# Adding the last sorted tiles of a mixture of experts to their tokens: through DRAM, or by products on chip

## The chip, the cores and the metric

The kernel runs on one core of one Trainium2 chip. The metric is the device time of one execution in microseconds, given as the median of several runs. The engines are PE (TensorE, matrix products), DVE (VectorE), ACT (ScalarE), POOL (GpSimd) and SP (SyncE, which here only issues transfers). Transfers run on the core's 16 DMA engines.

## The reference

The input is 2 sequences of 1024 tokens with 256 features, all in float32. An attention block with 16 heads of 128 (one shared key and value head) is followed by a mixture of experts. Both are modulated by shifts, scales and gates that depend on the sequence. Cut to what matters here:

```python
x = x + ga * attention(layernorm(x) * (1 + ca) + sa)
h = layernorm(x) * (1 + cb) + sb
logits = h @ router_w.T                      # 8 experts
topk_vals, topk_idx = top_k(logits, 2)
topk_w = softmax(topk_vals)
y1 = expert's w1 applied to h                # 2 * 176 columns
y2 = expert's w2 applied to silu(gate) * up  # 256 columns
y = sum over the two experts of topk_w * y2
out = x + gb * y
```

So each of the 2048 tokens has two expert results, which have to be weighted, multiplied by the gate `gb`, brought back to the token's place and added to the token's own row.

## The kernel before, in words

The tokens stand in 16 token tiles of 128 (`NT`), in four blocks of 512 (`NBLK`). `xs[:, t, :]` holds token tile `t` on chip for the whole run. The attention goes block by block, and PE works through 256 steps of a head and a key tile in each. Between these steps hooks, put there by `at(head, step, function)`, hand out the other work. One of them, in block 1, is `clear_sorted`: it fills the DRAM tensor `sorted_x` with zeros through SP's queue and writes into its rows the number of a row that no token owns.

The experts' stage works on sorted rows. Each row of a token (features, its weight in column `WEIGHT`, the row it belongs to in column `TO`) is scattered to `sorted_x`, so that the rows of one expert stand together in tiles of 128. There are `ALL` = 39 such tiles. `SETS` splits the token tiles in two: the first 12, and the last 4, which belong to the last attention block and are known only late. The sorted tiles from `ONES` = 32 on hold rows of the last four token tiles only.

One sorted tile is one object of class `Sorted`. Its stages are `turn` (transpose on PE, copy on ACT), `up` (product with w1, then ACT and DVE), `turn_back` (transpose) and `down` (product with w2). At the end of `down`, DVE evicts the product into `ysb` with weight and gate, and POOL issues an indirect DMA that scatters the 128 rows of `ysb` to the DRAM tensor `results`, two rows for each token. The loop over `m` runs these stages staggered. It takes 2.49 us a tile in the later part, and PE is always busy in it.

When the scatters that a token tile depends on have landed, `fetch` loads its two rows for each token from `results` (256 KB for a token tile). `combine` adds the two rows, adds the token's own row from `xs`, and stores the sum to the output. Scatters write rows of their own, so the class `Scattered` frees them of waits for each other; its `read` makes a load wait for the first `n` scatters. The loads of the first 12 token tiles wait for the first 32 scatters, those of the last 4 for all 39.

The order on each engine is made by a scheduler from the program's order and its own estimates. `tc.issue_after(i)` holds back what stands inside until instruction `i` has been issued on the planner's list. After the loop, five combines of the first set are put beside the last evictions (`BESIDE`). Then POOL, after its last scatter, writes a single column `sent`, and DVE copies it to `seen`. That copy stands ahead of the other seven combines of the first set. The last four loads go out on SP and ACT in turn, and four combines follow them.

Of the kernel before, what the change touches and what calls it, by code (L numbers as in the profile page):

```python
# [43 lines left out]
FP = mybir.dt.float32  # L44
I32 = mybir.dt.int32
AF = mybir.ActivationFunctionType
ALU = mybir.AluOpType
# [3 lines left out]
P = 128  # L51
# [9 lines left out]
def tile_adaln_attention_moe(  # L61
# [15 lines left out]
    nc = tc.nc  # L77
    B, N, D = x.shape
# [6 lines left out]
    QB = 512  # L85
# [9 lines left out]
    TOP = 2  # L95
    SETS = ((0, (NBLK - 1) * QT), ((NBLK - 1) * QT, NT))
# [3 lines left out]
    ONES = TOP * SETS[0][1] + E  # L100
    ALL = (TOP * NT * P + E * (P - 1)) // P
    PARTS = 3

    xt = x.rearrange("b (t p) d -> p (b t) d", p=P)
    ot = out.rearrange("b (t p) d -> p (b t) d", p=P)
# [6 lines left out]
    xs = keep.tile([P, NT, D], FP, name="xs")  # L112


    WEIGHT, TO, BATCH, ROW = D, D + 1, D + 2, D + 4
# [29 lines left out]
    for t in range(QT, TPB):  # L145
# [35 lines left out]
        base=0, channel_multiplier=0,  # L181
# [30 lines left out]
    results = dram.tile([(TOP * NT + ALL) * P, D], FP, name="results")  # L212
# [29 lines left out]
    into_results = Scattered("into_results")  # L242
# [4 lines left out]
    with ExitStack() as attn:  # L247
# [88 lines left out]

        def clear_sorted():

            zero = work.tile([P, ROW], FP, tag="h", name="zero")
            nc.vector.memset(zero, 0.0)  # L340
            by_tile = sorted_x.rearrange("(m p) d -> p m d", p=P)
            nc.sync.dma_start(out=by_tile, in_=zero.unsqueeze(1).to_broadcast([P, ALL, ROW]))
            nobody = work.tile([P, ALL, 1], I32, tag="z", name="nobody")
            nc.gpsimd.iota(nobody, [[P, ALL]], base=TOP * NT * P, channel_multiplier=1)
            with nc.allow_non_contiguous_dma(reason="one number of each row"):
                nc.sync.dma_start(out=by_tile[:, :, TO : TO + 1].bitcast(I32), in_=nobody)
# [175 lines left out]
        TWO = 2  # L522
# [885 lines left out]
        for blk in range(NBLK):  # L1408
# [78 lines left out]
            last = attention(blk, q, steps, besides)  # L1487
# [17 lines left out]
    with ExitStack() as moe:  # L1505
# [42 lines left out]
        class Sorted:  # L1548
# [45 lines left out]
            def down(self):  # L1594
                m = self.m
                at = expert(m) * (2 * D)
                y = ps_y.tile([P, D], FP, tag="y", name=f"sy_{m}")
                for c in range(2):
                    nc.tensor.matmul(  # L1599
                        y,  # L1600
                        self.actT[:, c, :],
                        w2_flat[:, c * D :][:, bass.ds(at, D)],
                        start=(c == 0),
                        stop=(c == 1),
                    )
                ysb = mg.tile([P, D], FP, tag="ysb", name=f"ysb_{m}", bufs=5)
                self.evicted = nc.vector.scalar_tensor_tensor(  # L1607
                    ysb, y, self.x[:, WEIGHT : WEIGHT + 1], self.gate, ALU.mult, ALU.mult
                )
                ins = nc.gpsimd.indirect_dma_start(  # L1610
                    out=results,
                    out_offset=bass.IndirectOffsetOnAxis(
                        ap=self.x[:, TO : TO + 1].bitcast(I32), axis=0
                    ),
                    in_=ysb,
                    in_offset=None,
                )
                self.scattered = ins.ins
                into_results.add(ins)

            def gates(self):

# [9 lines left out]
        def fetch(t, queue=nc.sync):  # L1632

            y = row_buffer(f"y_{t}").rearrange("p (k d) -> p k d", k=TOP)
            load = queue.dma_start(
                out=y,
                in_=results[TOP * t * P : TOP * (t + 1) * P, :].rearrange(
                    "(p k) d -> p k d", k=TOP
                ),
            )  # L1640
            into_results.read(load, ONES if t < SETS[0][1] else ALL)
            return y

        def combine(t, y, queue):

            sum_ = y[:, 0, :]
            nc.vector.tensor_tensor(sum_, sum_, y[:, 1, :], ALU.add)
            nc.vector.tensor_tensor(sum_, sum_, xs[:, t, :], ALU.add)
            queue.dma_start(out=ot[:, t, :], in_=sum_)

        settle.pools(mg, ms, ps_t, "t")
        gb_more = mg.tile([P, D], FP, name="gb_more", bufs=1)
        nc.vector.tensor_tensor(gb_more, gb[:, 1, :], gb[:, 0, :], ALU.subtract)
        tiles = []
        fetched, have = [], 0
        back = done = 0
# [9 lines left out]
            7: [lambda: count(NBLK - 1, mg, ps_t, "t"), lambda: place_second(mg, settle.shares)],  # L1666
        }
        SCATTERS = 8
        LATER = 24
        for m in range(ALL + 3):  # L1670
            there = ALL if m >= SCATTERS + TOP else FULL
            while len(tiles) < min(m + 1 + PRE, there):
                tiles.append(Sorted(len(tiles)))
            for f in late.get(m, ()):
                f()
            if m < ALL:
                tiles[m].turn()
            if 0 <= m - 1 < ALL:
                tiles[m - 1].up()
            sooner = m >= LATER  # L1680
            while back < min(m - 2 + sooner, ALL):
                tiles[back].gates()
                tiles[back].turn_back()
                back += 1
            while done < min(m - 3 + sooner, ALL):
                tiles[done].down()
                done += 1
            if SCATTERS <= m < SCATTERS + TOP:
                k = m - SCATTERS
# [12 lines left out]
        def added(some, behind, queue):  # L1702
            with tc.issue_after(behind):
                for t, y in some:
                    combine(t, y, queue)

        BESIDE = 5
        for i in range(BESIDE):
            m = ALL - 4 + i // 2
            added(  # L1710
                fetched[i : i + 1],
                tiles[m].evicted.ins if i % 2 else tiles[m + 1].active.ins,
                nc.sync,
            )
        sent = mg.tile([P, 1], FP, name="sent", bufs=1)
        with tc.issue_after(tiles[-1].scattered):
            nc.gpsimd.memset(sent, 0.0)
        seen = mg.tile([P, 1], FP, name="seen", bufs=1)
        with tc.issue_after(tiles[-1].evicted.ins):
            look = nc.vector.tensor_copy(seen, sent).ins  # L1720
        lasts = [(t, fetch(t, (nc.sync, nc.scalar)[t % 2])) for t in range(*SETS[1])]
        added(fetched[BESIDE:], look, nc.scalar)
        for t, y in lasts:
            combine(t, y, (nc.sync, nc.scalar)[t % 2])


_OUT = ((2, 1024, 256), "float32")
# [41 lines left out]
```

## Time and profile before

| | us |
|---|---|
| median of 3 runs | 1278.46 (1278.01 to 1279.04) |
| the profiled execution | 1271.44 |
| its span, first to last instruction | 1269.7 |
| PE busy in it | 1244.3 (98%) |
| DVE, ACT, POOL busy | 845.6, 454.2, 188.0 |
| last product of the experts ends | 1254.5 |

The profile is one execution, recorded instruction by instruction. A timeline row gives the start, the duration, the engine with the source line, what was written from what, and in brackets how long the engine had been idle and what ended that. The chain of waits follows the end back from the last instruction to what released each step. A row of a windows table gives the stretch, its length, the busy time of PE, PE's weight loads, DVE, ACT and POOL, then the granted clock of PE, the mean busy share of the DMA engines, and the GB/s that they moved. A transfer has two times: its issue, which is a short instruction of the issuing queue, and its landing.

### The profile page before, as it was taken

The numbers are of one execution on the slowest core, as the hardware profiler recorded it, in microseconds if no ns is written. First come the engines' busy times: TensorE is split into PE (matmuls) and PEld (weight loads), VectorE is DVE, ScalarE is ACT, GpSimd is POOL, SyncE is SP. The second block draws the span as 40 slices with busy tenths as digits, with TensorE's granted clock in tenths as the row PEclk, the third lists the DMA queues.
The fourth block names the chain that finished last, engine by engine and source line by source line (L and its number), as shares of the span: only waits on it lengthen the run. The fifth ranks groups of instructions, "written<-read, shape, count | busy, mean of one in ns | idle before, by whom it ended". The sixth has DMA issues, their size and how long they took to land.

```text
span 1269.7 us, 13438 instructions
## 1 busy us (share of the span) xinstructions
PE 1244.3 (98%) x4116; PEld 681.3 (54%) x4116; DVE 845.6 (67%) x1747; ACT 454.2 (36%) x887; POOL 188.0 (15%) x222
## 2 busy tenths in 40 slices
PE   8999999999999999999999999999999999999995
PEld 4544444457644444448545454448545454467773
DVE  6577789666866766665966666666857775547555
ACT  3533333431233334430333334331433343313431
POOL 3210323110000100000000000000000323203642
PEclk9999999999999999999999999999999999999997
DMA  8011031312011025111011111012011123212426
GB/s 265 0 34 34 9 88 22 91 22 72 7 43 52 30 94 142 34 34 34 13 51 38 33 34 34 33 34 96 13 50 38 59 94 115 67 34 81 151 84 236
DMA packets 87974, 79.25 MB, mean 62 GB/s; under 512 B 43520, under 2 KB 66688, under 8 KB 87648
## 3 DMA queue, kind: packets, MB, share of 16 engines
q1 hardware_dynamic: 82624, 67.06, 17.9%
q0 software_dynamic: 3408, 9.38, 2.0%
q10 hardware_dynamic: 1872, 1.97, 0.5%
q8 instruction: 33, 0.54, 0.2%
q14 instruction: 37, 0.30, 0.1%
HBM read 58.29 MB, written 20.08 MB: 62 GB/s over the span
## 4 chain that ended last, share of the span: by engine, by line
PE 86%; DVE 5%; DMA 3%; POOL 2%; issue 2%; SPq 1%; ACT 0%; POOLq 0%; ACTq 0%; DVEq 0%
PE s L741 32%; PE o L756 31%; PE pr L899 6%; PE q L667 6%; PE su L1574 3%; PE pr L820 2%; PE sy L1599 2%; PE q L616 1%; POOL rn_q L716 1%; DVE sum L761 1%; DMA y<-results 1%; PE kv L466 1%; DMA wide_q<-row_q 1%; DMA rT<-turned_r 1%; PE ap L1590 1%
## 5 line engine op out<-in xcount | busy, mean ns | idle before, releaser
L741 PE MATMUL s<-qT,kT 128*128 128x512 f32 x1024 | 524.4, 595 | 0.7 <-ACT qT L1284 0.7
L756 PE MATMUL o<-p,vs 128*128 128x512 f32 x1024 | 521.9, 592 | 1.0 <-ACT p L745 1.0
L745 ACT ACTIVATE p<-s 128x512 f32<-128x512 f32 x512 | 304.3, 597 | 505.5 <-PE s L741 489.9
L761 DVE TENSOR_TENSOR sum<-sum,p 128x512 f32<-128x512 f32 x384 | 263.8, 687 | 180.1 <-ACT p L745 178.2
L756 PEld LDWEIGHTS o<-p,vs 128*128 128x128 f32 x1024 | 194.0, 190 | 243.4 <-issue 236.5
L741 PEld LDWEIGHTS s<-qT,kT 128*128 128x128 f32 x1024 | 191.5, 190 | 190.2 <-issue 182.5
L716 POOL TENSOR_TENSOR rn_q<-rn_q,minus_half 128x16 f32<-128x16 f32 x15 | 44.0, 2935 | 411.7 <-DVE rn_q L712 363.6
L761 DVE TENSOR_TENSOR sum<-p,p 128x512 f32<-128x512 f32 x64 | 43.8, 684 | 44.3 <-ACT p L745 44.1
L534 DVE STREAM_TRANSPOSE turned_q<-sq_q 128x512 f32<-128x512 f32 x60 | 42.3, 705 | 26.3 <-ACT sq_q L629 26.3
L1574 PE MATMUL su<-w,xT 128*128 x156 | 52.8, 461 | 0.2
L899 PE MATMUL pr<-wout_sb,qT 128*128 128x128 f32 x384 | 50.0, 276 | 0.0
L566 DVE TENSOR_TENSOR qT<-qT,wide 128x512 f32<-128x512 f32 x64 | 43.5, 680 | 7.3 <-DMA wide<-row 6.9
L534 DVE STREAM_TRANSPOSE turned<-sum 128x512 f32<-128x512 f32 x64 | 45.4, 710 | 1.9
L1610 POOL DMA_INDIRECT results<-ysb,x x39 | 40.0, 1025 | 44.4 <-DVE ysb L1607 31.2
L899 PEld LDWEIGHTS pr<-wout_sb,qT 128*128 128x128 f32 x384 | 46.2, 192 | 0.1
L566 DVE TENSOR_TENSOR qT<-qT,wide_q 128x512 f32<-128x512 f32 x60 | 41.6, 694 | 6.1 <-DMA wide_q<-row_q 6.0
L763 ACT COPY qT<-o 128x512 f32<-128x512 f32 x64 | 37.4, 584 | 20.5 <-PE o L756 20.4
L535 DVE TENSOR_REDUCE parts<-turned 128x16 f32<-128x512 f32 x64 | 43.2, 675 | 1.2
L629 ACT ACTIVATE sq_q<-qT 128x512 f32<-128x512 f32 x50 | 31.4, 628 | 34.5 <-DVE qT L674 27.3
L535 DVE TENSOR_REDUCE parts_q<-turned_q 128x16 f32<-128x512 f32 x60 | 40.8, 680 | 1.0
L667 PE MATMUL q<-rows,wq_sb 128*128 128x256 f32 x150 | 40.5, 379 | 0.0
L1599 PE MATMUL sy<-w2s,sactT 128*128 x156 | 39.9, 380 | 0.0
(322 smaller groups left out, 1065.8 us busy)
## 6 DMA issues: line engine op xcount, KB each, us to landing
wide<-row SPq DMA_DIRECT2D x64, 256.0 KB, 3.9
wide_q<-row_q SPq DMA_DIRECT2D x60, 256.0 KB, 3.9
sorted_x<-zero SPq DMA_DIRECT2D x1, 5070.0 KB, 18.5
x<-sorted_x SPq DMA_DIRECT2D x39, 130.0 KB, 2.7
y<-results SPq DMA_DIRECT2D x14, 256.0 KB, 5.1
w<-in_w_dram SPq DMA_DIRECT2D x2, 1408.0 KB, 9.3
wout_sb<-in_wout_dram SPq DMA_DIRECT2D x1, 2048.0 KB, 17.7
wq_sb<-in_wq_dram SPq DMA_DIRECT2D x1, 1536.0 KB, 8.3
```

Of the source, the lines that this page charges most:

```text
L534: nc.vector.transpose(turned.rearrange("p c k -> p (c k)"), src)
L535: latest["vector"] = nc.vector.tensor_reduce(parts[:, i, :], turned, AX.X, ALU.add).ins
L566: nc.vector.tensor_tensor(q.head(h), q.head(h), wide, ALU.mult)
L667: nc.tensor.matmul(ps[:, k, :].rearrange("p (t k) -> p t k", k=P), x, y, start=True, stop=True,)
L716: latest["pool"] = nc.gpsimd.tensor_tensor(rn, rn, minus_half[:, :1].to_broadcast([P, SIDE // 2]), ALU.pow).ins
L741: latest["tensor"] = nc.tensor.matmul(s, kT[:, ts(b * NJ + j, P)], q.head(h), start=True, stop=True).ins
L745: nc.scalar.activation(p, s, AF.Exp)
L756: latest["tensor"] = nc.tensor.matmul(outs[h], vs[:, b * NJ + j, :], p, start=(j == 0), stop=(j == NJ - 1)).ins
L761: latest["vector"] = nc.vector.tensor_tensor(sums[h], first, p, ALU.add).ins
L899: nc.tensor.matmul(ps[:, piece, :], halves(g)[:, pair, head, t, i, :], w[:, g * HG // TWO + pair, :], start=False, stop=(g == NG - 1 and m ...
L1574: nc.tensor.matmul(u, self.xT[:, c, :], w1_flat[c][:, bass.ds(at, I2)], start=(c == 0), stop=(c == DC - 1),)
L1599: nc.tensor.matmul(y, self.actT[:, c, :], w2_flat[:, c * D :][:, bass.ds(at, D)], start=(c == 0), stop=(c == 1),)
```

## The change

The last three sorted tiles (`HERE` = 3: tiles 36, 37 and 38) are no longer scattered to DRAM. For each of them a new function `find` makes, from the column `TO`, the number of the token that each row belongs to, and compares it with a row of the numbers 1536 to 2047 (`tokens`). This gives a matrix `at` of 128 rows by 512 tokens with ones and zeros. After the loop, `bring` multiplies `at` (as weights) with `ysb`, which adds each row to its token in a PSUM tile `direct` of a token tile: three products, one for each sorted tile, for each of the four token tiles. DVE adds `direct` into `xs` before the last four combines.

The rows of `results` that would have held those rows now must be zero: `clear_sorted` gets a second store, of 1 MB of zeros, for the 1024 rows of the last four token tiles. The last four loads wait for the first 36 scatters, and all go out on SP.

Three combines of the first set (token tiles 9 to 11) move from DVE to POOL, after its last scatter, with their stores on ACT's queue. Nine stay on DVE: six are put beside the last evictions, three behind them. The column `sent` and its copy `seen` are gone.

```diff
+    HERE = 3
...
         def clear_sorted():
...
+            lo, hi = [TOP * t * P for t in SETS[1]]
+            nc.sync.dma_start(
+                out=results[lo:hi, :].rearrange("(m p) d -> p m d", p=P),
+                in_=zero[:, :D].unsqueeze(1).to_broadcast([P, (hi - lo) // P, D]),
+            )
...
             def down(self):
...
+                if m >= ALL - HERE:
+                    return
                 ins = nc.gpsimd.indirect_dma_start(
...
+            def find(self):
+                half = mg.tile([P, 1], I32, tag="half", name=f"half_{self.m}")
+                nc.vector.tensor_scalar(
+                    half, self.x[:, TO : TO + 1].bitcast(I32), 1, None, ALU.arith_shift_right
+                )
+                token = mg.tile([P, 1], FP, tag="token", name=f"token_{self.m}")
+                nc.vector.tensor_copy(token, half)
+                self.at = mg.tile([P, QB], FP, name=f"at_{self.m}", bufs=1)
+                nc.vector.tensor_scalar(self.at, tokens, token, None, ALU.is_equal)
...
-            into_results.read(load, ONES if t < SETS[0][1] else ALL)
+            into_results.read(load, ONES if t < SETS[0][1] else ALL - HERE)
...
-        def combine(t, y, queue):
+        def combine(t, y, queue, engine=nc.vector):
...
+        TOKENS, FIND = 20, 27
...
+            if m == TOKENS:
+                nc.gpsimd.iota(token_i, [[1, QB]], base=SETS[1][0] * P, channel_multiplier=0)
+                nc.vector.tensor_copy(tokens, token_i)
+            if FIND <= m - 4 < FIND + HERE:
+                tiles[m - 4 - FIND + ALL - HERE].find()
...
-        BESIDE = 5
-        for i in range(BESIDE):
...
-        sent = mg.tile([P, 1], FP, name="sent", bufs=1)
-        with tc.issue_after(tiles[-1].scattered):
-            nc.gpsimd.memset(sent, 0.0)
-        seen = mg.tile([P, 1], FP, name="seen", bufs=1)
-        with tc.issue_after(tiles[-1].evicted.ins):
-            look = nc.vector.tensor_copy(seen, sent).ins
-        lasts = [(t, fetch(t, (nc.sync, nc.scalar)[t % 2])) for t in range(*SETS[1])]
-        added(fetched[BESIDE:], look, nc.scalar)
-        for t, y in lasts:
-            combine(t, y, (nc.sync, nc.scalar)[t % 2])
+        lasts = [(t, fetch(t)) for t in range(*SETS[1])]
+        def bring(t, some):
+            i = t - SETS[1][0]
...
+                nc.tensor.matmul(
+                    direct[t],
+                    tile_.at[:, ts(i, P)],
+                    tile_.ysb,
+                    start=(tile_ is here[0]),
+                    stop=(tile_ is here[-1]),
+                )
+        here = tiles[ALL - HERE :]
+        for some in (here[:-1], here[-1:]):
+            for t in range(t0, t0 + TWO):
+                bring(t, some)
+        for t in range(t0 + TWO, t1):
+            bring(t, here)
+        OTHERS = 3
+        with tc.issue_after(tiles[ALL - HERE - 1].scattered):
+            for t, y in fetched[-OTHERS:]:
+                combine(t, y, nc.scalar, nc.gpsimd)
...
+        for i, (t, y) in enumerate(fetched[:-OTHERS]):
+            with tc.issue_after(behind[i] if i < len(behind) else last_at or tiles[-1].evicted.ins):
+                last_at = combine(t, y, nc.scalar if i >= len(behind) else nc.sync)
+        with tc.issue_after(last_at):
+            for t in range(t0, t1):
+                nc.vector.tensor_tensor(xs[:, t, :], direct[t], xs[:, t, :], ALU.add)
+            for t, y in lasts:
+                combine(t, y, (nc.sync, nc.scalar)[t % 2])
```

More of the change, by code (lines that the diff above doesn't have):

```diff
@@ L102, in tile_adaln_attention_moe @@
     PARTS = 3
+    HERE = 3
+    assert ALL - HERE >= ONES
     xt = x.rearrange("b (t p) d -> p (b t) d", p=P)
@@ L1606, in down @@
                 ysb = mg.tile([P, D], FP, tag="ysb", name=f"ysb_{m}", bufs=5)
+                self.ysb = ysb
                 self.evicted = nc.vector.scalar_tensor_tensor(
@@ L1640, in fetch @@
             )
-            into_results.read(load, ONES if t < SETS[0][1] else ALL)
+            into_results.read(load, ONES if t < SETS[0][1] else ALL - HERE)
             return y
-        def combine(t, y, queue):
+        def combine(t, y, queue, engine=nc.vector):
             sum_ = y[:, 0, :]
-            nc.vector.tensor_tensor(sum_, sum_, y[:, 1, :], ALU.add)
-            nc.vector.tensor_tensor(sum_, sum_, xs[:, t, :], ALU.add)
+            engine.tensor_tensor(sum_, sum_, y[:, 1, :], ALU.add)
+            last = engine.tensor_tensor(sum_, sum_, xs[:, t, :], ALU.add).ins
             queue.dma_start(out=ot[:, t, :], in_=sum_)
+            return last
         settle.pools(mg, ms, ps_t, "t")
@@ L1653, in tile_adaln_attention_moe @@
         nc.vector.tensor_tensor(gb_more, gb[:, 1, :], gb[:, 0, :], ALU.subtract)
+        token_i = mg.tile([P, QB], I32, name="token_i", bufs=1)
+        tokens = mg.tile([P, QB], FP, name="tokens", bufs=1)
         tiles = []
@@ L1699, in tile_adaln_attention_moe @@
         assert have == SETS[0][1] and done == ALL
[L1702 to L1705, printed above, removed]
-        BESIDE = 5
-        for i in range(BESIDE):
[L1709 to L1714, printed above, removed]
-        sent = mg.tile([P, 1], FP, name="sent", bufs=1)
@@ new lines, in tile_adaln_attention_moe @@
+        direct = {}
+        def bring(t, some):
+            i = t - SETS[1][0]
+            if t not in direct:
+                pool, tag = ((ps_u, "u"), (ps_t, "t"))[i // TWO]
+                direct[t] = pool.tile([P, D], FP, tag=tag, name=f"direct_{t}")
+            for tile_ in some:
+                nc.tensor.matmul(
[5 more added lines that the diff above has]
+                )
@@ new lines, in tile_adaln_attention_moe @@
+        here = tiles[ALL - HERE :]
+        t0, t1 = SETS[1]
+        for some in (here[:-1], here[-1:]):
[7 more added lines that the diff above has]
+                combine(t, y, nc.scalar, nc.gpsimd)
+        behind = [tiles[ALL - 4 + i // 2 + 1 - i % 2] for i in range(5)]
@@ new lines, in tile_adaln_attention_moe @@
+        behind = [a.evicted.ins if i % 2 else a.active.ins for i, a in enumerate(behind)]
+        behind += [tiles[ALL - 2].evicted.ins]
+        last_at = None
+        for i, (t, y) in enumerate(fetched[:-OTHERS]):
[6 more added lines that the diff above has]
+                combine(t, y, (nc.sync, nc.scalar)[t % 2])
```

## The prediction

> **What bounds the kernel now.** I read the page first: PE is busy 98% of the span, and the 40 slices show it full in all but the first and the last. So the first 1253 us are bound by PE, and the change adds nothing to PE there. What it rewrites is the last 15 us, after the last sorted tile, so the number has to come from there. I then read the chain of waits that ended last, for the window 1254 to 1270:
>
> ```profile
> 1255.77 1.27 POOLq L1765
> 1257.04 0.12 POOL sent L1717
> 1257.18 0.15 DVE seen L1720
> ...
> 1260.32 4.77 DMA y<-results
> 1265.09 0.02 issue
> 1265.11 0.44 DVE y L1647
> 1265.55 0.02 issue
> 1265.57 0.42 DVE y L1648
> ```
>
> The end hangs on the load of the last token tile (issued 1260.32, landed 1265.09) and two additions behind it; the last addition ends at 1265.99, its store lands and the span closes at 1269.7. What holds the loads? The timeline of POOL:
>
> ```profile
> 1251.28 0.96 POOL L1610 DMA_INDIRECT results<-ysb,x  x1 [1.53 <-DMA y<-results]
> 1253.54 0.96 POOL L1610 DMA_INDIRECT results<-ysb,x  x1 [1.31 <-DVE ysb L1607]
> 1254.81 0.96 POOL L1610 DMA_INDIRECT results<-ysb,x  x1 [0.30 <-issue]
> 1256.07 0.96 POOL L1610 DMA_INDIRECT results<-ysb,x  x1 [0.30 <-issue]
> ```
>
> These are the scatters of tiles 35 to 38. The last three are the ones that the change drops, so the loads would wait for the one of 1251.28 instead of the one of 1256.07: 4.8 us earlier by issue. But a load waits for the landing. I asked for the tile `results` in two windows that hold one scatter each, 1251:1252 and then 1256:1257:
>
> ```profile
> DMA to landing us min/median/max: 5.6/5.6/5.6
> ```
> ```profile
> DMA to landing us min/median/max: 2.9/2.9/2.9
> ```
>
> So tile 35 lands at 1251.28 + 5.6 = 1256.9 and tile 38 at 1256.07 + 2.9 = 1259.0: 2.1 us apart, not 4.8. The windows say why:
>
> ```profile
> 1246.00:1257.10 11.10, 8.52 (x41) 6.13 (x39) 6.78 (x18) 2.69 (x8) 5.81 (x7) 0.99 1.04 378
> 1257.10:1259.10 2.00, 0.00 (x0) 0.00 (x0) 1.92 (x7) 0.00 (x0) 0.05 (x1) 0.50 0.27 101
> 1259.10:1268.10 9.00, 0.00 (x0) 0.00 (x0) 5.97 (x17) 0.00 (x0) 0.00 (x0) 0.50 0.86 278
> ```
>
> The last two columns are the DMA engines' busy share and GB/s. They are full (1.04, 378 GB/s) until 1257.1 with the twelve loads of the first set, so an earlier scatter only queues longer. Then there is a hole of 2.0 us, which is all that the earlier start can win back, and after it 9 us at 278 GB/s.
>
> **The change part by part.** All sums are against the profiled execution (span 1269.7, 1271.44 us in all). The median of the runs shown is 1278.46, 7.0 us more; I carry differences over unchanged.
>
> *Loads of the last four token tiles.* First issue at 1256.9 + 0.15 (the delay after the landing of tile 38, 1259.0 to 1259.11) = 1257.05 instead of 1259.11: 2.06 earlier. All four now go through SP, 0.48 apart, so the fourth goes at 1258.5 (before: two queues, 1260.32). The first took 2.7 us to land, the last 1265.09 - 1259.11 = 6.0 us after the first issue, shared with seven stores. The same 6.0 gives 1263.0; if little competes, 1258.5 + 2.7 = 1261.2. On SP the loads stand among the six stores of the early additions; the waiting load can hold a store up to 2 us, but such a store has 8 us to the end. Cost nothing.
>
> *Scatters removed.* 3 x 128 KB of DMA and 3 x 1.26 us of POOL, with the memset and the copy that kept VectorE away: VectorE was idle 2.14 us there (`seen`), now gone.
>
> *Products.* 3 tiles x 4 token tiles = 12 products of 128x256. A `sy` pass (L1599) comes every 0.217 us (four in 0.87 in the chain), two passes a product, so 12 x 0.433 = 5.2 us on a PE that is idle after 1254.5: done by 1259.7, the third token tile at 1258.4. Cover: the loads land at 1261 to 1263. With that cover gone it would cost up to 5.2.
>
> *VectorE's end.* Additions of 128x256 follow each other at 0.335 us (two in 0.67 in the chain). Removed from VectorE: 3 combines = 6 x 0.335 = 2.0 us. Added: 4 additions from PSUM, 1.34 us. They are ordered after the last of the nine combines left, and before the four last combines (8 x 0.335 = 2.7). Call T the time at which those nine combines are done. Then VectorE's last addition ends at T + 1.34 + 2.7 + 0.1 = T + 4.1, if no load or product is later. Before it ended at 1265.99, so break-even is T = 1261.9. Undisturbed, VectorE has combines six to nine left at 1255, with one eviction: T = 1257.7; then the product of the fourth token tile (1259.7 + 0.42) governs and the end is 1262.9.
>
> *Three combines on GpSimd.* Six additions of 128x256 from about 1254.7, when the tenth load lands. Nearest row: the multiply of the same shape at L503, 0.73 us alone, 1.105 at most, so 4.4 to 6.6 us. Their stores queue on ACT, behind or ahead of VectorE's three; the last comes near 1261, still before the last token tiles' stores. The question is what they do to VectorE. Beside such a multiply the trace shows:
>
> ```profile
> 176.70 1.05 DVE L399 SCALAR_TENSOR_TENSOR h<-xs,mv_p,one_ca 128x256 f32<-128x256 f32 x1
> ```
> ```profile
> 176.74 0.72 POOL L503 TENSOR_TENSOR z<-z,norms_bc 128x256 f32<-128x256 f32 x1 [8.39 <-DVE z L411]
> ```
>
> Alone this instruction takes 0.49 (median of L404, the same kind). It ended 0.29 us after POOL did: it did its reading after POOL's. [...] By the row the two alternate: each of six GpSimd additions costs VectorE a turn, 0.73 + 0.30 = 1.03 us a pair, so T = 1254.7 + 6 x 1.03 = 1260.9 and the end is 1265.0. I take the row. Bounds: nothing (T = 1257.7) and 6 x 1.105 + 8 x 0.335 = 9.3 us (T = 1264.0).
>
> *Zeros for the second set's rows.* One more 1 MB store in block 1 behind the 5070 KB one. At that store's rate (5070 KB in 18.5 us) it is 3.7 us of DMA. SP's own waits there:
>
> ```profile
> SPq L346 <- DMA sorted_x<-zero: 18.1, 1, 18.1
> SPq L455 <- POOL rn_q L716: 10.5, 1, 10.5
> ```
>
> SP then waits 10.5 us for POOL before its next transfers, which hides the issue. The store of `nobody`, which takes 9.6 us, would end 3.7 us later, near 501.7 (issued 488.4), and the row broadcasts that SP issues from 499.4 may come some 1.5 us late; VectorE's multiplies of 505 to 511 use them. VectorE is 63% busy there and waits for ACT 6.0 us in 500 to 515, so I take zero; 1.5 us if that cover fails; a gain is excluded, since it only adds work.
>
> *Finding the rows.* Per tile two 128x1 operations (0.16 each) and a 128x512 comparison, estimated from L411's 0.41 at 256 elements as 0.67: 1.0 us, three times, in iterations of 2.49 us (near 1230 to 1238) where VectorE is busy 1.3. The activation multiply can come 0.7 us late, but PE reads it 1.6 us after. The iota on POOL (137 ns for 16 columns, 166 for 39, so an estimated 0.8 for 512) and its copy lie in gaps of 1.4 us between scatters. Zero; with cover gone, at most 1 us each.
>
> *Sum.* End of VectorE 1265.0 against 1265.99: -1.0 us, and the same store and close behind it. 1271.44 - 1.0 = 1270.4; as a median 1278.46 - 1.0 = 1277.5.
>
> **The rivals.** *The port hardly matters* (27%). [...] Then PE and the loads govern: last addition at 1262.9 (products) to 1263.9 (load at 1263.0 plus 0.88 for its two additions), a gain of 3.1 to 2.1, at best 1275.4. Against: the row beside L503.
>
> *GpSimd keeps VectorE from its end* (20%). One mechanism, the shared port, at its upper price: T = 1264.0, the last addition at 1268.1, slower by 2.1: 1280.6. It decides once T passes 1261.9, that is, once a GpSimd addition costs more than 1.2 us of VectorE's time. For it: L503 was 1.105 at most when VectorE ran densely, and VectorE is dense here. With block 1's 1.5 us on top it would be 3.6.
>
> *The change does not get its earlier start* (8%): the SP queue puts the waiting loads behind work that is late, or tile 35 lands as late as 1259. Then the loads keep their place and the result is within 0.5 us of before.
>
> **How the numbers follow.** My forecast has 45%: a gain of 0.2 to 2.2 us. 0.2% of the median is 2.56 us, about what a measurement of this kernel can tell from no change. Faster by more: most of the first rival and a little of the forecast, 0.27. Slower by more: three quarters of the second rival, with block 1's delay on top or a GpSimd addition dearer than any row of L503, and a little for what I don't see, 0.16. Between: 0.57. Range: from 3.1 faster, with 0.5 for the runs' own spread (1278.01 to 1279.04), to between the second rival's 2.1 and its 3.6 slower: 1274.9 to 1281.5.
>
> **What would show it.** Right: tile 35 lands near 1256.9, the four loads go at 1257 to 1258.5; VectorE's and POOL's additions alternate with VectorE rows near 1.0 us; PE's products end near 1260; the last addition near 1265. First rival: VectorE rows stay at 0.42 and PE or a load releases the last additions. Second: POOL rows over 1.1 and T after 1261.9. I am wrong altogether if PE shows idle time in 500 to 515, or if the loads start before 1256.

## The result and the profile after

| | before | after |
|---|---|---|
| median of the runs on one chip, us | 1278.28 (8 runs) | 1280.51 (8 runs) |
| the profiled execution, us | 1271.44 | 1279.91 |
| its span, us | 1269.7 | 1278.2 |

The change makes the kernel slower by 2.2 us: the ratio is 1.0021, with a 95% interval of 1.0011 to 1.0030. The forecast was 1277.5, 1.0 us faster.

The two profiled executions are 8.5 us apart, and most of that is not the change. Up to 1184 us both are in step. Then comes a stall, in the stretch in which `x` is loaded in bulk. The windows 1184 to 1200 of the kernel after, and of the kernel before from a second profile (experiment 1), with PE's busy time as the second number behind the stretch:

```profile
1184.00:1200.00 16.00, 9.66 (x36) 6.28 (x36) 4.19 (x11) 3.36 (x11) 8.65 (x9) 0.79 0.52 166
```
```profile
1184.00:1200.00 16.00, 10.88 (x42) 7.17 (x41) 4.75 (x12) 4.02 (x13) 9.29 (x11) 0.89 0.52 166
```

In the first profile of before, PE is busy 15.51 of these 16 us. So both kernels have the stall, 8.1 us of it in the change and 6.9 in that second profile of before; the first profile of before lacks it. PE's granted clock (third number from the right) is 0.79 and 0.89 in these two rows, and 1.00 in the first profile of before. To compare what comes behind it, count from the start of the 21st sorted tile's second product. From there to the end it takes 56.3 and 56.7 us in the two profiles of before, and 56.7 in the one of after. In its profile, then, the tail of the kernel after has won nothing.

Its chain of waits for 1260 to 1279 shows where the start that was won has gone:

```profile
1256.90 5.50 DMA y<-results
...
1262.57 0.72 POOL y L1671
...
1263.38 0.79 POOL y L1672
1264.17 0.02 issue
1264.19 0.36 ACTq L1673
...
1264.64 0.38 ACT sactT L1601
1265.02 0.04 issue
1265.07 1.15 PE sy L1608 x4
...
1266.24 0.48 DVE ysb L1617
```

Before, the chain went through the last scatters, `sent`, and the last load. Now a load of the first set, two additions on GpSimd and the issue of their store on ACT stand ahead of `sactT`, the copy of tile 38's hidden block, which has nothing to do with them. In ACT's program the store stands ahead of that copy, and in its timeline too:

```profile
1260.39 0.37 ACT L1601 COPY sactT<-ap 128x256 f32<-128x256 f32 x1
1264.19 0.36 ACTq L1673 DMA_DIRECT2D out_dram<-y  x1
1264.64 0.37 ACT L1601 COPY sactT<-ap 128x256 f32<-128x256 f32 x1 [3.88 <-DMA out_dram<-y]
```

Before, the same copy waited only for its own input:

```profile
1252.75 0.37 ACT L1592 COPY sactT<-ap 128x256 f32<-128x256 f32 x1 [0.71 <-PE ap L1590]
```

In the change ACT is idle 3.88 us between the copies of tiles 37 and 38. The bracket names the store as what ended the idle time: ACT was at the store, and the store was waiting for GpSimd. PE has no work meanwhile, and VectorE, which has to evict tile 38 before its next additions, waits for PE:

```profile
1261.22 1.03 PE L1608 MATMUL sy<-w2s,sactT 128*128 x4
1265.07 1.13 PE L1608 MATMUL sy<-w2s,sactT 128*128 x4 [2.82 <-ACT sactT L1601]
1266.03 5.34 PE L1744 MATMUL direct<-ysb,at 128*128 128x256 f32 x24
```
```profile
1266.24 0.48 DVE L1617 SCALAR_TENSOR_TENSOR ysb<-sy,x,gb 128x256 f32<-128x256 f32 x1 [1.80 <-PE sy L1608]
```

A smaller loss lies earlier. In the timeline of DVE, two of the three marks (`find`) stand waiting for the load of the `x` that they read, and PE's next transpose comes late behind the `sact` that was held up:

```profile
1223.52 0.15 DVE L1637 TENSOR_SCALAR half<-x 128x1 int32<-128x1 int32 x1 [1.54 <-DMA x<-sorted_x]
1229.06 0.15 DVE L1637 TENSOR_SCALAR half<-x 128x1 int32<-128x1 int32 x1 [1.12 <-DMA x<-sorted_x]
```
```profile
1230.22 0.44 PE L1599 MATMUL ap<-ident,sact 128*128 128x128 f32 x2 [0.39 <-DVE sact L1593]
```

### The profile page after: what moved, and what is told of

Same layout as the page of the kernel before. It is cut to its first block, busy times and chain, and to the rows that moved or that the text cites. A ratio compares the mean times of both kernels' runs of the same rounds, so it can differ in the third digit from the quotient of the medians.

```text
span 1278.2 us, 13487 instructions
## 1 busy us (share of the span) xinstructions
PE 1252.2 (98%) x4140; PEld 687.0 (54%) x4140; DVE 848.4 (66%) x1754; ACT 453.8 (36%) x887; POOL 191.0 (15%) x225
## 3 DMA queue, kind: packets, MB, share of 16 engines
q10 hardware_dynamic: 1440, 1.31, 0.3%
## 4 chain that ended last, share of the span: by engine, by line
PE 84%; DVE 6%; POOL 4%; issue 3%; DMA 2%; ACT 0%; SPq 0%; POOLq 0%; DVEq 0%; ACTq 0%
PE s L750 32%; PE o L765 31%; PE pr L908 6%; PE q L676 6%; PE pr L829 2%; PE q L625 1%; POOL results L1622 1%; PE su L1583 1%; PE sy L1608 1%; DVE sum L770 1%; PE kv L475 1%; POOL rn_q L725 1%; DMA wide_q<-row_q 1%; POOL sorted_x L1236 1%; DVE h L413 0%
## 5 line engine op out<-in xcount | busy, mean ns | idle before, releaser
L1622 POOL DMA_INDIRECT results<-ysb,x x36 | 37.4, 1040 | 50.7 <-DVE ysb L1617 40.0
```

## The experiments

The theory after this reading: the store on ACT ahead of `sactT` and the marks eat what the earlier loads bring. Rivals: GpSimd's additions, beside which three of VectorE's took 0.88 to 0.95 us in place of 0.42; and the stall near 1190 us, if the change made it longer. A ratio below is always to the kernel before, run beside it on the same chip. Experiments 1 to 4 ran on one chip, 5 to 7 on a second, 8 to 10 on a third, 11 to 13 on a fourth, 14 and 15 on a fifth. Differences between ratios of different chips carry the errors of both.

### 1. The kernel before once more

No edit.

> The kernel before once more, unchanged, for a second profile of it. Its first profiled execution took 1271.44 us, 7 us less than its own plain runs, and TensorE has no idle stretch there between 1186 and 1199 us; the profile of the changed kernel has three (0.71, 1.31 and 4.15 us) and is 8.07 us behind by then. Theory A (the stall belongs to both kernels and the first profile happened to miss it): the second profile shows a span near 1276, with the gaps at 1186 to 1199 us. Theory B (the stall came with the change): the second profile has no gap there and a span near 1270 again, though the plain run takes 1278.

Measured: 1279.57 us, span 1277.9, with the gaps (its window is shown above). Theory A. The stall goes with where the kernel runs: all seven profiles of experiments 1 to 7, from the two chips on which the kernel before took 1278.6 to 1278.8 us, have it, of either kernel and every variant, and none of the eight from the three chips on which it took 1270.9 to 1271.8. Each chip was measured at one time only, so chip and time are not told apart. What makes the stall was not settled. In it ACT starts nothing for up to 5.1 us (in the profile of the change) and then four ready instructions in a row within 1.1 us; the DMA share is 0.52 over 1184 to 1200 us, and 0.94 from 1192.3 to 1195.8.

### 2. GpSimd's stores behind the copy

```diff
-                combine(t, y, nc.scalar, nc.gpsimd)
+                combine(t, y, nc.scalar, nc.gpsimd, tiles[-1].copied)
...
-            queue.dma_start(out=ot[:, t, :], in_=sum_)
+                with tc.issue_after(store_behind):
+                    queue.dma_start(out=ot[:, t, :], in_=sum_)
```

> The changed kernel, with one thing moved: the stores of the three sums that GpSimd makes are issued on ACT behind the copy of the last tile's hidden block (sactT of tile 38), not ahead of it. Theory A (ACT stands 3.88 us at the first such store before it can copy): the copy comes near 1260.8 on the clock of the changed kernel's profile, the second product of tile 38 some 2.8 us earlier, TensorE's last products end near 1268.6 in place of 1271.4, and the time falls by 2 to 2.8 us against the changed kernel, to about 0.9995 of the kernel before. Rival (VectorE's sharing with GpSimd sets the end): the copy comes earlier but the last additions on VectorE stay where they are, less than 0.5 us gained.

Measured: 1279.27 against 1278.76, ratio 1.0006 (0.9996 to 1.0016). ACT's wait and PE's gap are gone: the second product of tile 38 follows that of tile 37 at once. That is some 1.9 us better than the change by the ratios, less than the 2.8 that the gap held. The timeline shows what came in its place, VectorE and GpSimd taking turns:

```profile
1259.72 0.72 POOL L1671 TENSOR_TENSOR y<-y 128x256 f32<-128x256 f32 x1 [1.61 <-DMA y<-results]
1259.85 0.88 DVE L1672 TENSOR_TENSOR y<-y,xs 128x256 f32<-128x256 f32 x1
1260.52 0.79 POOL L1672 TENSOR_TENSOR y<-y,xs 128x256 f32<-128x256 f32 x1
1260.64 0.94 DVE L1671 TENSOR_TENSOR y<-y 128x256 f32<-128x256 f32 x1
```

Alone such a VectorE addition takes 0.42 us. Five take 0.83 to 0.94 here and one 0.55. In the change only three are stretched, since VectorE stood waiting for PE through much of GpSimd's work. So the block on ACT had hidden most of the stretching.

### 3. No additions on GpSimd

```diff
-        OTHERS = 3
-        with tc.issue_after(tiles[ALL - HERE - 1].scattered):
-            for t, y in fetched[-OTHERS:]:
-                combine(t, y, nc.scalar, nc.gpsimd)
...
-        for i, (t, y) in enumerate(fetched[:-OTHERS]):
+        for i, (t, y) in enumerate(fetched):
```

> The changed kernel without GpSimd's additions: VectorE makes all twelve sums of the first token tiles, six additions of about 0.42 us more, and no store on ACT waits for GpSimd ahead of the copy. Theory A (the store on ACT): the copy of tile 38 is free again, 2.8 us earlier; VectorE has 2.5 us more of its own, less the roughly 1.5 us by which its additions beside GpSimd were stretched; about 1.5 to 2.5 us faster than the changed kernel. [...]

Measured: 1278.92 against 1278.76, ratio 1.0001 (0.9993 to 1.0010), 2.5 us better than the change. GpSimd's additions took six from VectorE, 2.5 us at 0.42, and stretched the others in experiment 2 by 2.6 (the six rows sum to 5.1 us where they would take 2.5). No gain of the move is seen even with the store out of the way.

### 4. The marks four steps later

```diff
-        TOKENS, FIND = 20, 27
+        TOKENS, FIND = 20, 31
```

> The changed kernel, with the three marks of tokens (half, token, at) made four steps later on VectorE (the step count 27 becomes 31), when the loads of their tiles have been in for microseconds. Theory A (they wait 1.54 and 1.12 us for a load and hold up the sact behind them): TensorE's gap of 0.39 us near 1230 is gone and the time falls by about 0.6 us. Rival (they cost nothing, the 0.6 us is the stretch of the stall before it): within 0.2 us of the changed kernel.

Measured: 1282.36 against 1278.76, ratio 1.0027 (1.0017 to 1.0037). The edit had no effect: the scheduler orders by its own estimates, and the order on all five engines came out as in the change. So this is the change measured again, and it confirms the loss. Beside it on the same chip experiments 2 and 3 are 3.1 and 3.4 us faster, and neither interval overlaps with this one (that of experiment 2 ends 0.0001 short of it): this is the clearest sign of what the store costs. Its profile is 1276.53, the lowest of its 15 runs, which left a question: the profiles of this kernel show a tail no longer than that of before, and its plain runs are 2 to 3.6 us slower.

### 5. The front parts alone, in the kernel before

The zeros, the token numbers and the marks added to the kernel before, their results unused; the tail unchanged.

```diff
+            nc.sync.dma_start(
+                out=results[lo:hi, :].rearrange("(m p) d -> p m d", p=P),
...
+            if m == TOKENS:
...
+                tiles[m - 4 - FIND + ALL - HERE].find()
```

> The kernel before, with the parts of the change added that lie ahead of the last tiles, and their results left unused: zeros written into the last four token tiles' part of results, the row of token numbers, and the three marks half, token, at for tiles 36 to 38. Scatters, loads and additions stay as before. Theory A (the marks wait for the x loads of their tiles on VectorE and hold up one sact): 0.6 us slower than the kernel before, with a gap of about 0.4 us on TensorE near the mark of tile 38; the zeros cost nothing. Rival (the zeros or the marks make the stall of the bulk x loads near 1186 to 1199 us longer): 2 us slower or more. If the prediction's zero for all three holds: within 0.3 us of the kernel before.

Measured: 1279.69 against 1278.60, ratio 1.0008 (0.9998 to 1.0018): 1.1 us at the middle, not told apart from nothing by itself. In its profile the tiles slip by 1.4 us where the marks stand. The stall takes 8.2 us in it, 8.1 in the change: no sign that these parts make it longer than in a kernel without them (6.9 in experiment 1) beyond what it varies anyway (6.5 between the profiled spans of experiments 6 and 13, 1275.3 and 1268.8 us, of one kernel with it and without).

### 6. The marks behind an eviction, no GpSimd additions

On top of experiment 3:

```diff
-                tiles[m - 4 - FIND + ALL - HERE].find()
+                with tc.issue_after(tiles[done - 1].evicted.ins):
+                    tiles[m - 4 - FIND + ALL - HERE].find()
```

> The changed kernel without GpSimd's additions (VectorE makes all sums, so no store on ACT waits ahead of the last copy), and the three marks are put on VectorE behind the eviction of an earlier tile, microseconds after the loads that they read have landed. Moving them by a step count alone did not move them: the planner put them at the same place. Theory A: 0.6 us faster than the same kernel with the marks where they were, about 0.9997 of the kernel before, and no gap on TensorE at the marks. Rival (the marks cost nothing in a plain run): the same time, 1.0001 of the kernel before.

Measured: 1277.54 against 1278.60, ratio 0.9990 (0.9983 to 0.9998). PE has no gap at the marks, and the tiles from the 21st to the 37th run in step with before, to 0.02 us. By the ratios of experiments 3 and 6 the marks were worth 1.4 us, more than the 0.6 expected, but these are two chips, the intervals overlap, and experiment 13 makes it 0.3. In the profiles that leave the marks where they were, the tiles slip by 0.15 to 1.44 us there, as the loads of `x` come earlier or later.

### 7. The tokens' own rows through TensorE

```diff
+                nc.tensor.matmul(direct[t], ident, xs[:, t, :], start=True, stop=False)
...
-                nc.vector.tensor_tensor(xs[:, t, :], direct[t], xs[:, t, :], ALU.add)
```

> As the one before it, and the last four token tiles' rows of xs are brought into direct by TensorE too, as products with the identity (four more products of about 0.44 us), so that VectorE's four additions xs<-direct (1.41 us in all) fall away at the end of its queue. Theory A (VectorE's queue sets the end once nothing blocks ACT): 1.2 to 1.4 us faster than the one before it, about 0.9987 of the kernel before. Rival (TensorE becomes the bound with 1.8 us more of products): the gain is under 0.5 us, and VectorE waits for the last direct.

Measured: 1277.74 against 1278.60, ratio 0.9991 (0.9984 to 0.9998), no gain over experiment 6. The size is the rival's, the cause is not: VectorE's queue is shorter, and it now waits for a load, not for a product:

```profile
1269.08 0.42 DVE L1671 TENSOR_TENSOR y<-y 128x256 f32<-128x256 f32 x1 [0.86 <-DMA y<-results]
```

### 8. The change with the marks behind

The edit of experiment 6 on the changed kernel, nothing else.

> The changed kernel with nothing but its three marks (half, token, at) put on VectorE behind the eviction of an earlier tile, after the loads that they read. GpSimd's additions and their stores on ACT stay as in the change. Theory A (marks about 1.1 us, the store on ACT about 2.5 us, the rest of the change about -1.1 us): 1 us or a little more faster than the changed kernel, some 1.0012 of the kernel before; TensorE's gap at the marks is gone and the one of 2.8 us ahead of the second product of tile 38 is still there. Rival (marks and store cost the same time twice, since VectorE's and ACT's delays overlap): no faster than the changed kernel.

Measured: 1272.93 against 1271.39, ratio 1.0009 (1.0002 to 1.0015), by the ratio 1.5 us better than the change, which was measured on other chips; the intervals overlap with the first result's and touch that of experiment 11. Its profile shows what the first one had not. The gap behind the store is 3.48 us, and what comes after it on PE is slow:

```profile
1258.05 2.07 PE L1608 MATMUL sy<-w2s,sactT 128*128 x4 [3.48 <-ACT sactT L1601]
1259.92 7.31 PE L1745 MATMUL direct<-ysb,at 128*128 128x256 f32 x24
```

In the windows of that run the third column from the right is PE's granted clock:

```profile
1254.60:1257.00 2.40, 0.00 (x0) 0.00 (x0) 1.17 (x4) 0.00 (x0) 1.43 (x2) 1.00 1.06 388
1257.10:1263.80 6.70, 5.75 (x14) 4.58 (x15) 3.10 (x8) 0.37 (x1) 2.86 (x5) 0.50 0.80 254
1264.00:1266.00 2.00, 2.00 (x11) 1.74 (x11) 0.88 (x3) 0.00 (x0) 0.00 (x0) 1.00 0.41 143
```

PE's clock fell to 0.50 about 2.5 us after its last product ahead of the gap, and stayed there for 6.8 us: 0.9 us more for the second product and 2.0 for the 24 passes of `direct` than in the profile of the change, where the gap was 2.82 us and the clock stayed:

```profile
1262.30:1265.00 2.70, 0.00 (x0) 0.00 (x0) 2.14 (x4) 0.36 (x1) 2.35 (x3) 1.00 1.02 374
1265.00:1271.40 6.40, 6.31 (x28) 5.24 (x28) 5.06 (x13) 0.01 (x1) 2.15 (x4) 1.00 0.86 285
```

The slow products reach VectorE, which waits for `direct` twice, 0.88 and 0.87 us; in the profile of the change it does not wait for it:

```profile
1265.97 0.42 DVE L1776 TENSOR_TENSOR xs<-direct,xs 128x256 f32<-128x256 f32 x1 [0.87 <-PE direct L1745]
```

The gap's length follows the load for GpSimd's first sum: GpSimd's first addition starts 1.94 us after tile 37's second product here, and 1.35 in the change.

### 9. Both: marks behind, stores behind

Experiments 2 and 8 together.

> The one before it, and the stores of GpSimd's three sums are issued on ACT behind the copy of tile 38's hidden block. Theory A: 2 to 2.5 us faster than the one before it, some 0.9993 of the kernel before, and TensorE has no gap ahead of the second product of tile 38. Rival (GpSimd's additions, whose sharing with VectorE stretched six of its additions from 0.42 to 0.83 to 0.94 us when the store was moved, take the gain back): less than 1 us faster than the one before it, and slower than the same kernel without GpSimd's additions (0.9990).

Measured: 1271.08 against 1271.39, ratio 0.9998 (0.9990 to 1.0006), 1.4 us better than experiment 8 by the ratios: more than the rival's 1 us and less than theory A's 2. GpSimd's additions stay. Whether they take back a part is not told apart from nothing, since without them (experiments 6 and 13) the ratio is 0.9990 and 0.9999.

### 10. The last four loads on two queues

On top of experiment 7:

```diff
+        with tc.issue_after(tiles[-1].copied):
+            lasts = [(t, fetch(t, (nc.sync, nc.scalar)[t % 2])) for t in range(*SETS[1])]
```

> No additions on GpSimd, marks behind, xs of the last four token tiles brought in by TensorE, and the last four loads issued two on SP and two on ACT (behind the copy of tile 38), where SP alone issued them over 2.2 us and VectorE then waited 0.86 us for the second. Theory A (VectorE's queue and then those loads set the end): 0.5 to 1 us faster than with the loads on SP alone, 0.9985 of the kernel before. Rival (the last products or the last stores set the end): the same as with the loads on SP alone, 0.9991.

Measured: 1270.71 against 1271.39, ratio 0.9994 (0.9988 to 1.0000). No better than experiment 7, so the loads' issue is not what is left.

### 11. The change once more

No edit, on a chip without the stall.

> The changed kernel once more, unchanged, beside the next two. Its two profiles so far (the second as the run with the marks moved by a step count, which left every engine's order the same) show a tail within 0.4 us of the kernel before, where its plain runs are 2 to 3.6 us slower. Theory A (in most runs TensorE's gap ahead of tile 38's second product is long enough that its granted clock falls to a half, as in the run with the marks behind: a gap of 3.48 us, then 0.50 from 1258 to 1264 us and the products in 7.31 us in place of 5.34): 2 to 3.5 us slower than the kernel before. Rival (the excess was the stall of the bulk x loads on those chips): within 1 us of the kernel before on a chip without the stall.

Measured: 1273.15 against 1270.88, ratio 1.0021 (1.0015 to 1.0028). So the loss is not the stall. Its profile has the gap with 3.20 us, and half the clock for 3.4 us behind it, from 0.6 us after PE had work again:

```profile
1257.53 1.49 PE L1608 MATMUL sy<-w2s,sactT 128*128 x4 [3.20 <-ACT sactT L1601]
1258.81 6.72 PE L1744 MATMUL direct<-ysb,at 128*128 128x256 f32 x24
```
```profile
1257.50:1258.10 0.60, 0.57 (x3) 0.52 (x4) 0.00 (x0) 0.00 (x0) 0.60 (x2) 1.00 0.62 219
1258.20:1261.50 3.30, 3.30 (x10) 2.59 (x9) 2.38 (x7) 0.00 (x0) 1.31 (x2) 0.50 0.92 242
```

### 12. The gap filled

Six products that nobody reads, ahead of tile 38's second product:

```diff
+                if m == ALL - 1:
+                    idle = ps_t.tile([P, D], FP, tag="t", name="idle")
+                    for _ in range(6):
+                        nc.tensor.matmul(idle, ident, tiles[m - 3].ysb, start=True, stop=True)
```

> The changed kernel, with six products of 0.44 us on TensorE between the second products of tiles 37 and 38, whose output nobody reads. They fill 2.7 us of the gap in which TensorE waits for ACT's copy, and change nothing else; the store on ACT still stands ahead of the copy. Theory A (the lost clock is part of the cost): 1 to 2.5 us faster than the changed kernel, granted clock 1.00 throughout the tail, the 24 products of direct in 5.34 us. Rival (only the late copy costs): no faster than the changed kernel, or slower by what the six products delay the second product of tile 38.

Measured: 1273.37 against 1270.88, ratio 1.0019 (1.0012 to 1.0025). Not a clean experiment, so it does not tell what the clock costs: the clock stayed at 1.00, but the scheduler had moved the eviction of tile 38 behind seven more additions, and PE waited for it:

```profile
1261.61 0.48 DVE L1621 SCALAR_TENSOR_TENSOR ysb<-sy,x,gb 128x256 f32<-128x256 f32 x1
1262.15 3.72 PE L1748 MATMUL direct<-ysb,at 128*128 128x256 f32 x16 [1.69 <-DVE ysb L1621]
```

### 13. Experiment 6 on a chip without the stall

No further edit.

> The version without GpSimd's additions and with the marks behind, beside the changed kernel in the same call. It measured 0.9990 of the kernel before elsewhere. Theory A (the change is worth about -1.1 us without its marks' wait, the store on ACT and GpSimd's sharing): 0.9987 to 0.9995 of the kernel before and 3 to 5 us faster than the changed kernel. Rival (its gain was a matter of the stall near 1190 us): 1.0000 of the kernel before on a chip without the stall.

Measured: 1271.25 against 1270.88, ratio 0.9999 (0.9991 to 1.0007), by the ratios 2.8 us better than the change beside it on the same chip, and the intervals do not overlap. Against the kernel before the gain of experiment 6 was not found again; the two intervals share 0.9991 to 0.9998.

### 14. The gap filled, VectorE's order held

Experiment 12, and the addition that follows the eviction of tile 38 in the change is held behind it by `tc.issue_after(tiles[-1].evicted.ins)`.

> The changed kernel with the six filling products between the second products of tiles 37 and 38, as tried before, but with VectorE's order held as in the changed kernel up to the last four token tiles: with the filling products alone the planner had moved the eviction of tile 38 behind five additions of VectorE (ysb at 1261.61 in place of 1258.6 us), which took the gain back. Theory A (the late copy and the lost clock each cost something): TensorE's granted clock stays at 1.00, the products of direct take 5.3 us in place of 6.7, and the time is 0.7 to 1.5 us below the changed kernel's 1.0021 of the kernel before, about 1.0012. Rival (the clock costs nothing because VectorE and the stores follow later anyhow): 1.0019 to 1.0024.

Measured: 1272.72 against 1271.83, ratio 1.0008 (0.9999 to 1.0017), 1.7 us better than the change by the ratios; the change was not run on this chip, and its interval and that of experiment 11 overlap by 0.0002. ACT's copy is as late as ever, and PE's clock behind the filling is 1.00:

```profile
1258.58 1.13 PE L1612 MATMUL sy<-w2s,sactT 128*128 x4 [1.06 <-ACT sactT L1601]
1259.55 5.34 PE L1752 MATMUL direct<-ysb,at 128*128 128x256 f32 x24
```
```profile
1258.50:1264.80 6.30, 6.22 (x28) 5.24 (x28) 4.95 (x13) 0.03 (x1) 2.07 (x3) 1.00 0.91 267
```

By the ratios filling the gap gains about as much as moving the store (1.7 and 1.9 us), each known to about 1 us. That would make the lost clock most of what the store costs, but it is not shown: the chips differ, the order of the last four tiles' additions differs too, and in its profile the tail from the 21st tile's second product takes 57.6 us, no less than the 57.2 of experiment 11.

### 15. The token numbers behind too

The cast of the token numbers was put by the scheduler not at the 21st step but among the additions of the last block's norm, on the path to the first tiles. In the change's profile:

```profile
1155.43 0.42 DVE L1706 CAST tokens<-token_i 128x512 f32<-128x512 int32 x1
1155.77 0.42 DVE L997 TENSOR_TENSOR proj<-proj,gg 128x256 f32<-128x256 f32 x1
```
```profile
1159.62 0.44 PE L1599 MATMUL ap<-ident,sact 128*128 128x128 f32 x2 [0.83 <-DVE sact L1593]
```

Edit on top of experiment 6:

```diff
+                with tc.issue_after(tiles[done - 1].evicted.ins):
                     nc.gpsimd.iota(token_i, [[1, QB]], base=SETS[1][0] * P, channel_multiplier=0)
                     nc.vector.tensor_copy(tokens, token_i)
```

> The version without GpSimd's additions and with the marks behind, and the row of token numbers (iota on GpSimd, its cast on VectorE) is put behind the eviction of an earlier tile too. In the changed kernel the planner put the cast (0.42 us) at 1155.43 us into the chain of the last block's norm, and TensorE's gap at 1159 us is 0.83 us in place of 0.52. Theory A: the gap is 0.52 us again and the time falls by 0.3 us against that version, to 0.9990 to 0.9994 of the kernel before (1.0 us faster or somewhat less). Rival (the cast costs nothing): the same as that version, 0.9990 and 0.9999 in its two measurements.

Measured: 1270.13 against 1271.83, ratio 0.9986 (0.9977 to 0.9995), 1.7 us faster than before. With experiments 6 and 7 it is one of three versions whose interval lies below 1, all of which keep the products and drop the additions on GpSimd; it was measured once, and experiment 6's gain was not found again in experiment 13. The gap is back where it was:

```profile
1160.16 0.33 PE L1599 MATMUL ap<-ident,sact 128*128 128x128 f32 x1 [0.54 <-DVE sact L1593]
```

The 0.3 us are thus shown in the profile. Whether they show in the runs is not told apart from the spread between experiments 6 and 13.

## Why the prediction was wrong

**The step that failed** is the sentence on the three stores: they "queue on ACT", their last one near 1261, "still before the last token tiles' stores". It asked when the stores would be done and not what stands behind them. One of them stands ahead of `sactT` of tile 38, on the path of everything that followed: ACT idle 3.88 us, PE 2.82 to 3.48. With the store moved behind the copy (experiment 2) the time falls by some 1.9 us against the first result, and by 3.1 against the change beside it (experiment 4).

**What the gap does to PE** was in none of the cases. With 2.82 us, and 2.64 in experiment 4, the clock stayed at 1.00; with 3.20 in experiment 11 and 3.48 in experiment 8 it fell to 0.50. How long PE had been idle when it fell differs. In the first profile of before the clock fell 2.5 us after PE's last product, which the prediction's own windows show (PE idle after 1254.5, a clock of 0.50 from 1257.1), and in the change 2.8 us after it. In experiment 8 it fell 2.5 us into the gap, in experiment 11 0.6 us after the gap had ended, 3.8 us after it had begun, and in the stall of the change 0.6 us into the longest gap there (4.15 us). So the runs give no length from which a single gap loses the clock, and whether another gap of 2.82 us would keep it is not shown.

How many plain runs lost their clock can be read from the mean granted clock that is on record for each run. In the profile of experiment 11 PE's last product ends 5.7 us before the end; half the clock in what follows could not bring the mean below 0.998. Of the 21 runs of the change there, 14 have 0.996 or 0.997; beside them, one of 13 in experiment 13, which has no gap, and none of 21 in experiment 12, where it is filled. So most runs of the change on this chip lost their clock before the last product. These 14 take 1273.35 us at the median and the other seven, one of which (the profiled one) lost it too, 1272.22. So the lost clock goes with about 1 us; a load that lands late could lengthen both. Experiment 14 puts it at 1.7 us, experiment 12 saw no gain. How the store's cost divides between the late copy and the clock stays open.

**The marks** were taken at nothing, "with cover gone, at most 1 us each". The cover named, PE's 1.6 us, does not cover an instruction that waits: the prediction costed what the marks do (the three 128x512 comparisons took 0.48, 0.64 and 0.49, not the estimated 0.67), not what they wait for. In the profiles they cost 0.15 to 1.44 us; by the ratios 1.4 us (experiments 3 and 6) or 0.3 (3 and 13). **The iota and its copy** too were taken at nothing: 0.3 us of PE's gap (0.83 in place of 0.52), in a place that the step number in the source does not tell. From the end of the attention's last product (`pr`) to the start of tile 0's second product it takes 8.86 us in both profiles of before, 9.17 in the change and 8.87 in experiment 15.

**What held.** The scatters removed and the earlier loads: the first of the last four loads was issued at 1265.06 in the change, 3.8 us after tile 37's second product began; before, it was 6.6 us after, and the prediction had it at 4.6. The zeros for `results` cost nothing: the profiles are in step through block 1, and PE is full from 500 to 515 (15.00 of 15 us) before and after. The products took 5.34 us for 5.2. The alternation of VectorE and GpSimd is there once the store is out of the way, at 0.90 us a turn in experiment 9 where 1.03 was taken. There the last addition ends 50.9 us after the 21st tile's second product began; the prediction's 1265.0 is 51.6 on the same count. So the sum for the tail agrees with the profile of a kernel in which the store and the marks cost nothing: from the 21st tile's second product to the end that one takes 55.4 us, 0.9 and 1.3 less than the two profiles of before. Its runs, 0.9998 (0.9990 to 1.0006), exclude neither the forecast's 1.0 us nor no gain at all. In the changed kernel itself only three additions of VectorE were stretched.

**The rivals.** The one on the slower side had the size (2.1 us) and not the cause: GpSimd's additions did not keep VectorE from its end, it waited 1.80 us for PE. That the measured 1280.5 lies within the stated range is therefore luck. The case that GpSimd's additions hardly slow VectorE's is refuted by the stretched rows of experiments 2 and 9. No run shows the shared port that both rivals name, nor which engine reads first; what the runs show is that five of six VectorE additions beside GpSimd's take 0.83 to 0.95 us there, where one alone takes 0.42.

**The profile against the median.** Carrying the difference over unchanged from 1271.44 to 1278.46 was right: of the 8.1 us between the two profiles of before, the stall makes 6.9, and no sign was found that this change touches it.

| version | ratio to before |
|---|---|
| the change | 1.0021, 1.0027, 1.0021 |
| marks behind | 1.0009 |
| gap filled, VectorE's order changed | 1.0019 |
| gap filled, VectorE's order held | 1.0008 |
| the kernel before with the front parts alone | 1.0008 |
| stores behind | 1.0006 |
| no additions on GpSimd | 1.0001 |
| marks and stores behind | 0.9998 |
| marks behind, none on GpSimd | 0.9990, 0.9999 |
| the same, the tokens' rows through TensorE | 0.9991, 0.9994 |
| marks and token numbers behind, none on GpSimd | 0.9986 |

These steps do not add up to one sum: a shorter gap can also be a gap without a lost clock, the store's delay had hidden that by GpSimd's additions, and the chips differ.

## What to carry to other kernels

When an operation moves to another engine, follow its output transfer too: the store that waited here on ACT's queue held ACT for 3.88 us, so ask which instruction stands next in that queue and who waits for it. Cost an added instruction by what it waits for as well as by its duration, and look in the engine's real order for its place, since a scheduler may put it elsewhere than the source does. Where PE is idle only once, a gap can cost twice, as in experiment 8: 3.48 us itself, and 2.9 us by the clock in the products behind it; ask for the clock in the windows behind each gap, also when the gap looks short.

## What the runs showed of the hardware that was not expected

- The stall near 1190 us, of 6.9 us in the profile of experiment 1 and 8.1 in that of the change, with the same kernel at 1278.8 us on one chip and 1270.9 on another. Its cause stays open; it is in no profile of the three chips on which the kernel before took under 1272 us.
- Half the granted clock after an idle stretch of 3.20 us in one run and of 3.48 in another, and none after 2.82 and 2.64. The low stretch lasted 3.4 us in the first and 6.8 in the second. After PE's last product the clock fell 2.5 us later in the first profile of before and 2.8 in that of the change. In the stall of the change it fell 0.6 us into an idle stretch of 4.15 us, behind two of 0.71 and 1.31, and was 0.50 for 6.8 us.
- Two engines that add in turn, 128x256 each: 0.72 to 0.96 us on GpSimd, 0.83 to 0.95 on VectorE (0.55 for one of six, in experiments 2 and 9) in place of 0.42. Six additions given away cost VectorE as much as they saved.
